# Handing the first pair of each conditional part of a two-round MoE loop to the part in front of it

## The chip, the cores and the metric

The kernel runs on one core of a Trainium2 chip. The metric is the device time of one execution in microseconds; the time of a kernel is the median of several runs. TensorE (PE) does the matrix products and the transposes, VectorE (DVE) and ScalarE (ACT) the elementwise work, GpSimd (POOL) issues the indirect transfers (gathers and scatters by a list of row numbers), and SyncE (SP) issues the direct ones.

## The reference, cut to what matters

The input is 2 x 2048 tokens of 512 numbers. A linear-attention layer comes first and then a mixture of experts (MoE): 32 experts, 8 chosen per token, hidden width 192, everything in float32.

```python
# x: [4096, 512] after the attention layer and its residual, layer-normed
logits = x @ wg.T
weights, idx = top_k(softmax(logits), 8);  weights /= weights.sum(-1)
for each (token, expert) of the 8 x 4096, sorted by expert:
    h = silu(x[token] @ w1[expert]) * (x[token] @ v1[expert])     # 512 -> 192
    out[token] += weight * (h @ w2[expert])                       # 192 -> 512
result = x1 + layernorm(out)
```

How many tokens each expert gets is known only while the kernel runs.

## The kernel before, in words

**Blocks and pairs.** The routing writes, for each expert, a list of its tokens. The lists are cut into blocks of 128 tokens of one expert, and two blocks make a *pair*. The tiles of a pair carry `s` = 0 or 1 for its two blocks. Round 1 has 24 pairs (`NP1`) that are known before the attention is finished; round 2 has up to 120 (`NP2`). The pairs of round 2 are numbered from 0 here.

**`prepare` (L666 to L689)** gets a pair ready. For each of its two blocks SP reads the expert's number (L671) and issues the weights: `w1t` (L674, 768 KB) and `w2t` in two pieces (L675 and L676, 256 and 128 KB). Each has three buffers per block (`NR` = 3), so that the load for pair n waits until pair n-3 has been computed. POOL gathers the 128 token rows into `xg` (L679; four buffers, which are two pairs). PE turns them with four transposes into PSUM, `px` (L685; two buffers), and DVE copies them to SBUF as `xgT` (L687; six buffers).

**`run_pair` (L691 to L729)** computes it. In the records each float32 matrix product counts as two PE instructions. For each block there are 8 PE instructions for `pgu` (L698), then Silu on ACT (L701) and the product `hh` on DVE (L702). Three transposes `ph` (L710) and one copy `hT` (L712) serve both blocks. `py` (L715 four instructions, L719 four) is the second product. ACT scales it by the routing weight (`ysb`, L723) and POOL adds the rows to the accumulators in HBM with an indirect transfer (L724).

**Parts.** Round 2 is cut into parts of 104, 8, 2, 2, 2 and 2 pairs (`PARTS`, L77). Part 0 always runs; each later part sits in an `If` on the number of pairs, `np2`, nested in the one before (L759 to L763). In the profiled execution 138 pairs run in all, 24 in round 1 and 114 in round 2: parts 0, 1 and 2. `second_round` (L749) prepares its first pair, and then for each pair prepares the next one and runs the present one. The first pair of a part has no pair in front of it within the part. So `prepare` of pair 104 is the first thing in the body of part 1, and that of pair 112 the first in part 2.

**Order of the work.** SP's order is the order of the program (`manual_schedule`, L664). For the other engines the framework fixes the order when the kernel is compiled: it goes through a stretch of code, takes for each engine the work that stands earliest in the program among what it reckons to be ready, and lets later work fill in where the earlier is not. The body of an `If` is planned as a stretch of its own, and nothing is moved into it or out of it. On the chip each engine then works strictly in this order, and waits where its next instruction is not ready. There is no common barrier at an `If`: each engine reads `np2`, compares and goes on.

**The end.** After the last part the final stage (L767 to L789) reads both accumulators, normalizes, adds `x1` and stores.

Of the kernel before, what the change touches and what calls it, by code (L numbers as in the profile page):

```python
# [8 lines left out]
F32 = mybir.dt.float32  # L9
# [8 lines left out]
P = 128  # L18
# [5 lines left out]
def linear_attention_then_moe(  # L24
# [24 lines left out]
    C = HID // P  # L49
# [23 lines left out]
    NP2 = (NB - N1 + 1) // 2  # L73
# [3 lines left out]
    PARTS = [(NT * K // BS - N1) // 2, 8, 2, 2, 2, 2]  # L77
# [6 lines left out]
    xn_d = dram.tile([NT + P, HID], F32, name="xn_d")  # L84
# [562 lines left out]
    with ExitStack() as mctx:  # L647
        plan = mctx.enter_context(tc.tile_pool(name="plan", bufs=1))
# [4 lines left out]
        hp = pairs.enter_context(tc.tile_pool(name="hp", bufs=3))  # L653
# [9 lines left out]
        w2v = w2r.rearrange("r (c h) -> (r c) h", c=FC)  # L663
        pairs.enter_context(tc.manual_schedule(engines={mybir.EngineType.SP}))  # L664

        def prepare(r, cols, tid, wt, load, xsrc):  # L666

            xgTs = []
            for s, c0 in enumerate(cols):
                w1t, w2t = w1b[s][r], w2b[s][r]  # L670
                ld = nc.sync.value_load(load[:, c0 : c0 + 1], min_val=0, max_val=2 * E - 1)  # L671
                ex = ld & (E - 1)
                skip = {"cond": ld < E, "bounds_check": "skip_entire_dma"}
                nc.sync.dma_start(w1t, wgu[bass.ds(ex * P, P), :], **skip)  # L674
                nc.sync.dma_start(w2t[:, 0, :], w2v[bass.ds(ex * F + s * FR, P), :], **skip)  # L675
                nc.sync.dma_start(w2t[s * FR : (s + 1) * FR, 1, :],  # L676
                                  w2v[bass.ds(ex * F + (1 - s) * P, FR), :], **skip)
                xg = xg_p.tile([P, HID], F32, tag="xg", name="xg")
                nc.gpsimd.indirect_dma_start(  # L679
                    out=xg, out_offset=None, in_=xsrc,  # L680
                    in_offset=bass.IndirectOffsetOnAxis(ap=tid[:, c0 : c0 + 1], axis=0),
                )
                px = ps_a.tile([P, C, P], F32, tag="xt", name="px")
                for c in range(C):
                    nc.tensor.transpose(px[:, c, :], xg[:, c * P : (c + 1) * P], ident)  # L685
                xgT = hp.tile([P, C, P], F32, tag="xgT", name="xgT", bufs=6)
                nc.vector.tensor_copy(xgT, px)  # L687
                xgTs.append(xgT)
            return xgTs  # L689

        def run_pair(r, cols, tid, wt, load, xgTs):  # L691

            hh = hp.tile([P, 2, F], F32, tag="hh", name="hh")
            for s, xgT in enumerate(xgTs):
                w1t = w1b[s][r]
                pgu = ps_a.tile([P, F2], F32, tag="gu", name="pgu")
                for c in range(C):
                    nc.tensor.matmul(pgu, xgT[:, c, :], w1t[:, c * F2 : (c + 1) * F2],  # L698
                                     start=(c == 0), stop=(c == C - 1))
                hs = hp.tile([P, F], F32, tag="hs", name="hs")  # L700
                nc.scalar.activation(hs, pgu[:, :F], AF.Silu)  # L701
                nc.vector.tensor_mul(  # L702
                    hh[:, s, :].rearrange("p (k c) -> p c k", c=FC),
                    hs.rearrange("p (c k) -> p c k", c=FC),
                    pgu[:, F:].rearrange("p (c k) -> p c k", c=FC),
                )
            hf = hh.rearrange("p s f -> p (s f)")
            ph = ps_a.tile([P, 3, P], F32, tag="ht", name="ph", bufs=1)
            for c in range(3):
                nc.tensor.transpose(ph[:, c, :], hf[:, c * P : (c + 1) * P], ident)  # L710
            hT = hp.tile([P, 3, P], F32, tag="hT", name="hT")
            nc.vector.tensor_copy(hT, ph)  # L712
            py = [ps_a.tile([P, HID], F32, tag="y", name=f"py{s}") for s in range(2)]
            for s in range(2):
                nc.tensor.matmul(py[s], hT[:, 2 * s, :], w2b[s][r][:, 0, :],  # L715
                                 start=True, stop=False)
            for s in range(2):
                rows = slice(s * FR, (s + 1) * FR)
                mm = nc.tensor.matmul(py[s], hT[rows, 1, :], w2b[s][r][rows, 1, :],  # L719
                                      start=False, stop=True)  # L720
            for s, c0 in enumerate(cols):
                ysb = hp.tile([P, HID], F32, tag="ysb", name="ysb")
                nc.scalar.activation(ysb, py[s], AF.Copy, scale=wt[:, c0 : c0 + 1])  # L723
                sc = nc.gpsimd.indirect_dma_start(  # L724
                    out=acc_d[s][:, :],
                    out_offset=bass.IndirectOffsetOnAxis(ap=tid[:, c0 : c0 + 1], axis=0),
                    in_=ysb, in_offset=None, compute_op=ALU.add,
                )
            return mm, sc  # L729

        done = []
        for i in range(NP1):
            pair = (i % NR, (i, NP1 + i), *(a[:, 0, :] for a in round1[:3]))
            done.append(run_pair(*pair, prepare(*pair, xn_d[: SNAP * TB, :])))
# [6 lines left out]
        np2 = plan.tile([P, 1], I32, name="np2")  # L741
        nc.vector.tensor_copy(np2, round2[3])
        np2 = nc.values_load(np2[:1, :], min_val=0, max_val=NP2)

        def pair2(i):
            g, jj = divmod(i, GP2)
            return (NP1 + i) % NR, (jj, GP2 + jj), *(a[:, g, :] for a in round2[:3])

        def second_round(i0, n):  # L749
            ready = prepare(*pair2(i0), xn_d[:, :])  # L750
            for i in range(i0, i0 + n):
                if i % 3 == 0 and i // 3 < NTILE:
                    t = i // 3
                    nc.sync.dma_start(x1_sb[:, t, :], x1_d[t * P : (t + 1) * P, :])
                now, ready = ready, prepare(*pair2(i + 1), xn_d[:, :]) if i + 1 < i0 + n else None
                run_pair(*pair2(i), now)

        second_round(0, PARTS[0])
        with ExitStack() as asked:  # L759
            for k in range(1, len(PARTS)):  # L760
                i0 = sum(PARTS[:k])
                asked.enter_context(tc.If(np2 > i0))
                second_round(i0, PARTS[k])  # L763
        pairs.close()


# [63 lines left out]
```

## Time and profile before

| | |
|---|---|
| time, median of 3 runs | 2855.16 us (2854.49 to 2856.72) |
| the profiled execution's own time | 2861.29 us |
| its span | 2859.5 us |
| mean granted clock of TensorE | 0.966 |
| PE busy over the span | 2645.8 us (93%) |
| first transposes of the MoE | 1342.5 us from the span's start |
| last pair's `py` begins | 2768.76 us |
| first read of the final stage | 2780.68 us |

The profile is of one execution. Positions are microseconds from the start of its span. In the view in order of time a row has start, duration, engine, line, operation, tile written and tiles read, count, and in brackets the idle time in front of it with what ended it. In the view of stretches a row has the stretch, its length, then the busy time and number of instructions of PE, PE's weight loads, DVE, ACT and POOL, the granted clock of PE, the busy share of the DMA engines, and GB/s. In the view of one line's instructions a row has the count and the shortest, median and longest duration in ns.

### The profile page before, as it was taken

Reading aid. Unit: us, or ns where it says so; the run is one execution under the profiler, and the core shown is the slowest. Engines: PE = TensorE matmul, PEld = TensorE weight load, DVE = VectorE, ACT = ScalarE, POOL = GpSimd, SP = SyncE. Lnnn points to the kernel's source line nnn. Section 1 sums busy time; section 2 is a strip of 40 time slices with the busy share of each in tenths; the row PEclk is TensorE's granted clock in tenths of the full one; section 3 lists DMA queues with packets and bytes.
Section 4 is the critical chain, followed back from the end, with each engine's and each line's share of the span. In section 5 each row is a group of like instructions: output and inputs, shape, how many; then the busy total and the mean of one; then the engine's idle time right before and its main releaser. Section 6 shows DMA issues by size and latency. Waiting matters only on the chain. (4 is left out here: it accounts for less than half of the span.)

```text
span 2859.5 us, 29618 instructions
## 1 busy us (share of the span) xinstructions
PE 2645.8 (93%) x8443; PEld 1310.7 (46%) x8443; DVE 1061.4 (37%) x2432; ACT 674.8 (24%) x1208; POOL 1059.9 (37%) x891
## 2 busy tenths in 40 slices
PE   8999999998999999998779899999999999999850
PEld 3434444444444444444435455555555555555420
DVE  5334544546533536554412222222222222222217
ACT  4332222213331313221211112121212121212114
POOL 1100223122320122223455555555555555554426
PEclk9999999999999999999889999999999999999985
DMA  3291211212111212123647899989787988685548
GB/s 112 86 329 51 68 52 52 68 52 67 37 56 45 71 34 71 53 71 114 161 102 175 212 268 257 274 200 254 165 214 160 314 194 199 137 194 114 104 87 323
DMA packets 179290, 399.83 MB, mean 140 GB/s; under 512 B 29413, under 2 KB 30438, under 8 KB 178610
## 3 DMA queue, kind: packets, MB, share of 16 engines
q0 software_dynamic: 70144, 145.31, 25.1%
q1 hardware_dynamic: 101602, 237.55, 24.9%
q10 hardware_dynamic: 7376, 15.02, 1.4%
q8 instruction: 70, 1.15, 0.2%
q14 instruction: 98, 0.80, 0.1%
HBM read 488.74 MB, written 116.66 MB: 212 GB/s over the span
## 5 line engine op out<-in xcount | busy, mean ns | idle before, releaser
L698 PE MATMUL pgu<-w1t,xgT 128*128 128x384 f32 x2208 | 780.0, 496 | 3.5 <-issue 2.4
L724 POOL DMA_INDIRECT acc_d<-ysb,tid x276 | 441.9, 1601 | 503.8 <-ACT ysb L723 389.5
L203 POOL DMA_INDIRECT list_d<-tw,pi x256 | 252.2, 985 | 979.6 <-DVE pi L201 556.2
L698 PEld LDWEIGHTS pgu<-w1t,xgT 128*128 128x128 f32 x2208 | 399.5, 191 | 327.2 <-issue 109.3
L552 PE MATMUL pq<-xlT,wq_sb 128*128 128x512 f32 x1024 | 463.1, 598 | 1.2 <-DVE sq L559 1.2
L584 PE MATMUL acc<-m,sq 128*128 128x512 f32 x1024 | 463.0, 597 | 0.0
L702 DVE TENSOR_TENSOR hh<-hs,pgu 128x192 f32<-128x192 f32 x276 | 97.3, 355 | 975.9 <-ACT hs L701 838.2
L723 ACT ACTIVATE ysb<-py,wt 128x512 f32<-128x512 f32 x276 | 176.5, 684 | 783.4 <-PE py L719 731.8
L679 POOL DMA_INDIRECT xg<-xn_d,tid x276 | 274.9, 996 | 119.0 <-PE px L685 64.0
L552 PEld LDWEIGHTS pq<-xlT,wq_sb 128*128 128x128 f32 x1024 | 190.7, 190 | 241.5 <-issue 230.8
L584 PEld LDWEIGHTS acc<-m,sq 128*128 128x128 f32 x1024 | 189.1, 190 | 239.6 <-issue 239.1
L715 PE MATMUL py<-w2t,hT 128*128 128x512 f32 x552 | 266.4, 605 | 2.1 <-issue 2.1
L555 ACT ACTIVATE qe<-pq,nbq_sb 128x512 f32<-128x512 f32 x128 | 87.8, 686 | 514.6 <-PE pq L552 509.0
L687 DVE COPY xgT<-px 128x512 f32<-128x512 f32 x276 | 188.3, 683 | 43.6 <-PE px L685 41.3
L559 DVE SCALAR_TENSOR_TENSOR sq<-pq,bq_sb,qe 128x512 f32<-128x512 f32 x128 | 95.8, 748 | 286.0 <-ACT qe L556 285.9
L685 PE MATMUL px<-ident,xg 128*128 128x128 f32 x1104 | 174.2, 284 | 29.1 <-DMA xg<-xn_d,tid 26.7
L701 ACT ACTIVATE hs<-pgu 128x192 f32<-128x192 f32 x276 | 90.3, 330 | 363.2 <-PE pgu L698 336.7
L685 PEld LDWEIGHTS px<-ident,xg 128*128 128x128 f32 x1104 | 135.9, 147 | 56.9 <-issue 32.0
L715 PEld LDWEIGHTS py<-w2t,hT 128*128 128x128 f32 x552 | 107.5, 196 | 109.2 <-issue 74.0
L719 PE MATMUL py<-w2t,hT 64*128 64x512 f32 x552 | 157.1, 642 | 0.0
L710 PE MATMUL ph<-ident,hh 128*128 128x128 f32 x414 | 100.5, 298 | 51.3 <-DVE hh L702 51.2
L469 PE MATMUL pk<-wk_sb,xlT 128*128 128x512 f32 x256 | 119.7, 607 | 0.0
(185 smaller groups left out, 1844.8 us busy)
## 6 DMA issues: line engine op xcount, KB each, us to landing
w1t<-in_wgu_dram SPq DMA_DIRECT2D x276, 768.0 KB
w2t<-in_w2r_dram SPq DMA_DIRECT2D x276, 256.0 KB
w2t<-in_w2r_dram SPq DMA_DIRECT2D x276, 128.0 KB
nb<-nr_d SPq DMA_DIRECT2D x128, 256.0 KB
acc_d<-zero SPq DMA_DIRECT2D x6, 2048.0 KB
xb<-in_x_dram SPq DMA_DIRECT2D x32, 256.0 KB
xr<-in_x_dram SPq DMA_DIRECT2D x32, 256.0 KB
wo<-in_woT_dram SPq DMA_DIRECT2D x32, 256.0 KB
```

The costliest lines, as they stand in the source:

```text
L203: nc.gpsimd.indirect_dma_start(out=list_d[:, :], out_offset=bass.IndirectOffsetOnAxis(ap=pi[:, k : k + 1], axis=0), in_=tw[:, k, :], in_of ...
L469: nc.tensor.matmul(pk, xlT[:, c, :], wk_sb[:, c, :], start=(c == 0), stop=(c == C - 1))
L552: nc.tensor.matmul(pq, wq_sb[:, c, h * P : (h + 1) * P], xlT[:, c, :], start=(c == 0), stop=(c == C - 1))
L584: nc.tensor.matmul(pa[s], a[:, s * P : (s + 1) * P], ms[h], start=(h == 0), stop=(h == H - 1))
L679: nc.gpsimd.indirect_dma_start(out=xg, out_offset=None, in_=xsrc, in_offset=bass.IndirectOffsetOnAxis(ap=tid[:, c0 : c0 + 1], axis=0),)
L685: nc.tensor.transpose(px[:, c, :], xg[:, c * P : (c + 1) * P], ident)
L687: nc.vector.tensor_copy(xgT, px)
L698: nc.tensor.matmul(pgu, xgT[:, c, :], w1t[:, c * F2 : (c + 1) * F2], start=(c == 0), stop=(c == C - 1))
L715: nc.tensor.matmul(py[s], hT[:, 2 * s, :], w2b[s][r][:, 0, :], start=True, stop=False)
L719: mm = nc.tensor.matmul(py[s], hT[rows, 1, :], w2b[s][r][rows, 1, :], start=False, stop=True)
L723: nc.scalar.activation(ysb, py[s], AF.Copy, scale=wt[:, c0 : c0 + 1])
L724: sc = nc.gpsimd.indirect_dma_start(out=acc_d[s][:, :], out_offset=bass.IndirectOffsetOnAxis(ap=tid[:, c0 : c0 + 1], axis=0), in_=ysb, in_ ...
```

## The change

`prepare` gets an argument `into`: the two tiles that receive the turned token rows, in place of two from the rotating `xgT`. Two pairs of such tiles, `ahead`, of 2 KB per partition each, are allocated in the pool `plan`, which stays open to the end. `second_round` no longer prepares its own first pair. It is handed the pair that is ready, and in its last turn it prepares the first pair of the *next* part into `ahead[k % 2]` before it runs its own last pair. That `prepare` stands in the body of the part in front, outside the `If` of the part that will use it. It holds all the instructions of `prepare`: two reads of the expert's number and six weight transfers on SP, two gathers on POOL, eight transposes on PE and two copies on DVE. The first pair of part 0 is prepared where it was. The last part that runs now prepares a pair as well, which no part then computes, if there is a next part at all.

```diff
-        def prepare(r, cols, tid, wt, load, xsrc):
+        def prepare(r, cols, tid, wt, load, xsrc, into=None):
...
-                xgT = hp.tile([P, C, P], F32, tag="xgT", name="xgT", bufs=6)
+                xgT = into[s] if into else hp.tile([P, C, P], F32, tag="xgT", name="xgT", bufs=6)
...
-        def second_round(i0, n):
-            ready = prepare(*pair2(i0), xn_d[:, :])
+
+        ahead = [[plan.tile([P, C, P], F32, name=f"ahead{k}{s}") for s in range(2)] for k in range(2)]
+
+        def second_round(k, ready):
+            i0, n = sum(PARTS[:k]), PARTS[k]
             for i in range(i0, i0 + n):
                 if i % 3 == 0 and i // 3 < NTILE:
                     t = i // 3
                     nc.sync.dma_start(x1_sb[:, t, :], x1_d[t * P : (t + 1) * P, :])
-                now, ready = ready, prepare(*pair2(i + 1), xn_d[:, :]) if i + 1 < i0 + n else None
+                now, ready = ready, None
+                if i + 1 < i0 + n:
+                    ready = prepare(*pair2(i + 1), xn_d[:, :])
+                elif i + 1 < NP2:
+                    ready = prepare(*pair2(i + 1), xn_d[:, :], ahead[k % 2])
                 run_pair(*pair2(i), now)
-
-        second_round(0, PARTS[0])
+            return ready
+
         with ExitStack() as asked:
-            for k in range(1, len(PARTS)):
-                i0 = sum(PARTS[:k])
-                asked.enter_context(tc.If(np2 > i0))
-                second_round(i0, PARTS[k])
+            ready = prepare(*pair2(0), xn_d[:, :])
+            for k in range(len(PARTS)):
+                if k:
+                    asked.enter_context(tc.If(np2 > sum(PARTS[:k])))
+                ready = second_round(k, ready)
```

## The prediction

> **What bounds the kernel now.** The page comes first. PE is busy for 93% of the span, so only what shortens PE's work or its idle time counts. Next is the view in stretches around the two places where a part ends and the next begins.
>
> ```profile
> 2637.51:2648.20 10.69, 9.28 (x28) 3.63 (x26) 1.27 (x3) 1.92 (x4) 3.12 (x2) 1.00 0.42 56
> 2648.20:2658.04 9.84, 0.00 (x0) 0.00 (x0) 0.00 (x0) 1.26 (x2) 7.00 (x6) 0.75 0.64 114
> 2658.04:2670.49 12.45, 12.23 (x48) 8.46 (x49) 5.16 (x9) 0.66 (x2) 5.32 (x6) 0.79 0.40 124
> 2699.14:2718.12 18.98, 18.98 (x71) 10.31 (x70) 4.80 (x10) 3.85 (x8) 6.97 (x5) 1.00 0.53 84
> 2738.55:2747.79 9.24, 0.00 (x1) 0.00 (x0) 0.00 (x0) 1.26 (x2) 6.72 (x6) 0.68 0.63 117
> 2747.79:2759.06 11.27, 10.44 (x38) 6.80 (x38) 4.03 (x7) 0.66 (x2) 0.27 (x1) 0.81 0.15 44
> ```
>
> Inside a part PE has no idle time: 18.98 of 18.98 us for two pairs, so 9.49 us a pair. At the boundaries (2648.20 and 2738.55) it does nothing for 9.84 and 9.24 us, and then runs at a mean clock of about 0.8. The rows in order of time say what it waits for.
>
> ```profile
> 2647.06 1.13 PE L719 MATMUL py<-w2t,hT 64*128 64x512 f32 x4
> 2649.18 1.56 POOL L724 DMA_INDIRECT acc_d<-ysb,tid  x1 [4.32 <-ACT ysb L723]
> 2651.04 1.56 POOL L724 DMA_INDIRECT acc_d<-ysb,tid  x1 [0.30 <-issue]
> 2652.91 1.02 POOL L679 DMA_INDIRECT xg<-xn_d,tid  x1 [0.30 <-issue]
> 2654.23 0.98 POOL L679 DMA_INDIRECT xg<-xn_d,tid  x1 [0.30 <-issue]
> 2658.04 3.87 PE L685 MATMUL px<-ident,xg 128*128 128x128 f32 x16 [9.86 <-DMA xg<-xn_d,tid]
> 2661.71 3.54 PE L698 MATMUL pgu<-w1t,xgT 128*128 128x384 f32 x8
> 2665.08 0.38 PE L685 MATMUL px<-ident,xg 128*128 128x128 f32 x2
> 2665.30 2.75 PE L698 MATMUL pgu<-w1t,xgT 128*128 128x384 f32 x8
> 2670.49 1.88 PE L715 MATMUL py<-w2t,hT 128*128 128x512 f32 x4
> ...
> 2743.26 1.01 POOL L679 DMA_INDIRECT xg<-xn_d,tid  x1 [0.30 <-issue]
> 2747.79 4.04 PE L685 MATMUL px<-ident,xg 128*128 128x128 f32 x16 [9.24 <-DMA xg<-xn_d,tid]
> 2751.62 5.54 PE L698 MATMUL pgu<-w1t,xgT 128*128 128x384 f32 x16
> 2759.06 1.98 PE L715 MATMUL py<-w2t,hT 128*128 128x512 f32 x4
> ...
> 2768.76 1.96 PE L715 MATMUL py<-w2t,hT 128*128 128x512 f32 x4 [0.70 <-issue]
> ```
>
> The chain at 2648 is: `py` of pair 103 ends, ACT scales, POOL issues two scatters, and only then the gathers, since POOL works in order. The first gather starts at 2652.91 and has landed by 2658.04, 5.13 us later (4.53 at the second boundary). The 16 transposes are those of pairs 104 and 105. Weights are no part of it: the rows of SP in order of time show loads for pair 106 at 2646.30, so SP is long past the `If`.
>
> **The change, part by part.** *Reference.* I write py(n) for the start of `py` of pair n. Before: py(101) 2627.75, py(103) 2645.17, py(104) 2670.49, py(105) 2681.44, py(106) 2689.64, py(107) 2699.14. From 101 to 107 that is 71.39 us against 6 x 9.49 = 56.94, so boundary 1 costs 14.4 us in all. That is the ceiling there.
>
> *`prepare` of pair 104 moved into part 0.* On SP its loads come in the same order as before, so nothing is moved past anything. On POOL its two gathers now stand in front of the scatters of pairs 101 to 103. There POOL has room: between 2607 and 2649 it waits 3 to 6 us in front of each pair of scatters. Without that cover they would cost two rows of 0.98 us plus 0.30 each, 2.6 us. On DVE two copies of 0.69 us fall where it is mostly idle. On PE eight transposes enter the tail of part 0, which had none. With them py(102) should come one full period after py(101), at 2637.24 (before 2637.51). Then 12 `pgu` instructions follow where there were 8: steady rows give 7.0 us from `py` to their end, and the old tail gives 1.94 us from there to the next `py`. So py(103) is at 2646.2, and its end at 2649.2 instead of 2648.19: **1.0 us later**, with the scatters and gathers behind it.
>
> *What PE finds in part 1.* `pgu` of pair 104 has tokens and weights, so 8 instructions can run at once, to 2652.1. The next question decides the case: where the transposes of pair 105 stand in PE's order. In the program they come before `run_pair(104)`, so they go first once the planner reckons the gather landed. What it reckons is seen in the old part 1: it put two transposes of pair 106 between the two `pgu` groups of pair 104, although pair 106 comes *after* `run_pair(104)` in the program, and its gathers were the fifth and sixth of the body. It thinks gathers quick. Now the gathers of 105 are the first of the body, and I take their transposes to stand after some 8 to 10 `pgu` instructions, within the second group. PE then stops there until the gather of 105 lands. That gather stands behind the scatters of pair 103 as the gather of 104 did: 2652.91 + 1.0 + 4.9 (between 4.53 and 5.13) = 2658.8. **This is the wait that takes the place of the old one**; behind it PE holds the rest of pair 104, and ACT, DVE and POOL its results.
>
> *Sum at boundary 1.* After a stop of 6 us or so I expect the slow clock again. The old row has 3.54 us for 8 `pgu` behind the wait against 2.75 for the next 8, and 16 transposes took 3.87. So from 2658.8: eight transposes in two groups 1.8, the remaining 6 to 8 `pgu` 3.1, then 1.94 to `py`: py(104) = 2665.6, a gain of 4.9. Three steady periods on, py(107) is at 2694.1, or 2694.8 if no `pgu` of 105 slipped in front of py(104); before 2699.14. **Gain 4.65 us** (4.3 to 5.0).
>
> *Boundary 2.* The tail is again 1.0 us longer, so the gather of 113 starts at 2744.3 and lands at 2749.0 (4.53 us, plus some tenths for the weights of pair 114, which are now under way). With the same 1.8 + 3.1 + 1.94, py(112) = 2755.9 against 2759.06: 3.2 gained. Then the waste: pair 114 is prepared and never computed. Its weights and gathers run beside other work (the DMA share is 0.15 there). If that cover were missing, two gathers would cost POOL 2.6 us. Its eight transposes lie partly in PE's waits for `hh` and `hT` at the tail; bounds 0 and 1.0 us, I take 0.5, so py(113) - py(112) = 10.2 (before 9.70), py(113) = 2766.1, **gain 2.7**. The end hangs on pair 113's scatters, so it moves with it.
>
> *Entering the part.* The branch now has less idle time around it.
>
> ```profile
> L759 PEldq COMPARE_BRANCH  x4: 65/142/3689, 2646.7 to 2772.8; - x4
> ```
>
> The two that go on into a body took 92 and 65 ns, while earlier `py` instructions were still in the array; I count 0.1 us each, inside the roundings. The 3689 ns one is the jump over the parts not asked for, at 2768.9. If each entry cost that, the wait for the gather would still cover it in this case.
>
> *Memory.* The tiles take 8 KB per partition of `plan` and move what is allocated behind it, the weight buffers too. The first weights wait for the attention's last product (a 23.2 us wait of SP that ends at 1335). A loss there is hardly possible, as all that lay there is free by then, and a gain is capped, as PE's first transposes wait for the gathers that POOL starts at 1336.1. Bounds -2 and 0 us, I take 0.
>
> *Total.* 4.65 + 2.7 = **7.3 us**. The profiled execution took 2861.29 us, its span 2859.5 and 1.8 around it; that is 6.1 us over the median, without idle time of another kind at the boundaries that I can see. So I take the gain off the median: 2855.2 - 7.3 = **2847.9 us**, -0.26%. About 0.2%, or 5.7 us, is what a measurement of this kernel can tell from no change.
>
> *A rule against it.* The Trainium skill, "TensorE: Matmul & The Clock Gate", Part 1, says that an idle window of about 3.4 us drops PE to half clock, and that it needs about 3.4 us of sustained work to come back. The rows agree in kind: clock 0.75 and 0.68 in the idle stretches, 0.79 and 0.81 after. By that rule a stop cut from 9.8 to 6 us wins nothing of the slow start, about 1.7 us a boundary as an estimate from the page; my sum has the slow start from the rows already and stays as it is.
>
> **The rivals.** *A2, the planner puts the transposes of 105 behind all 16 `pgu`.* Then they run to 2655 while the gather is under way. py(104) = 2658.8 + 1.8 + 1.94 = 2662.5 and py(107) 2691.7, a gain of 7.4; at boundary 2 it is 2749.0 + 1.8 + 1.94 + 10.2 = 2762.9, a gain of 5.9. Total 13.3: **2841.9 us**. Against it: the two early transposes of 106.
>
> *B, they stand behind py(104)*: the stop is gone. The old second boundary has 7.44 us from the first `pgu` to `py`, so py(104) = 2649.3 + 7.44 = 2656.7. With 3.0 of `py`, 1.5 for transposes and copy of 105, 7.44 again and 0.8 for other transposes, py(105) = 2669.4 and py(106) = 2678.9, a gain of 10.7. At the second boundary 2747.1 + 3.0 + 1.4 + 7.44 + 0.5 = 2759.4, a gain of 9.3. Total 20: **2835.2 us**. This needs a planner that knows of the scatters in front.
>
> *C, they stand in front of all of pair 104*: only the copy and half of the transposes are saved. py(104) = 2658.8 + 2.0 + 7.44 + 0.7 (slow clock) = 2668.9, and py(106) gains 1.5; boundary 2 loses 0.5. **2854.2 us**, no change. Against it: `pgu` of 104 is ready at once and nothing else is.
>
> *D, slower: the gather of 105 lands much later.* The last weights and the scatters share the DMA engines with it, and every microsecond of lateness goes into PE's stop at both boundaries, since PE stands in the middle of pair 104. My gain of 7.3 is spent when each lands 3.65 us later than I say, 8.5 us after its start. At 7.3 us later the kernel is 7.3 us slower: **2862.5 us**. For it: the DMA share is 0.64 in the idle stretch, and rises if pair 114's weights come there. Against it: the two landings seen, 5.13 and 4.53 us.
>
> **How the numbers follow.** Case A, the sum above, 52%; A2 13%; B 10%; C 12%; D 13%. Within A the clock and the tail can take 2 us either way, so some 7 in 10 of it lie beyond 5.7 us. Faster: 36 + 13 + 10 = 0.59. Same: 15 from A and 12 from C, 0.27. Slower: D and the last of A, 0.14. Range: from 2837.0 (A2 with 5 us of its own for clock, tail and memory; most of B left out) to 2856.0 (C and 2 us; most of D left out), which leaves out some 19%.
>
> **What would show it.** At 2649 a PE row of `pgu` with no wait in front; some 8 to 10 instructions later transposes with a wait of about 6 us for `xg`; py(104) near 2665.6, and py(112) near 2751.2, which is 2755.9 less the gain of boundary 1. The step on the order is wrong if that wait is missing (B), or is the first thing in the body (C). The step on POOL is wrong if the gather does not start 1.9 us after the last scatter of the part in front. The tail's 1.0 us is wrong if py(103) stays at 2645.2.

## The result and the profile after

The changed kernel takes **2853.02 us** (median of 12 runs, 2846.9 to 2856.86); the kernel before took 2854.70 us beside it (median of 12 runs, 2852.82 to 2859.73). The ratio is 0.999, with an interval of 0.9981 to 0.9999. That is 1.7 us, 0.06%, inside the 0.2% that count here as no change. The forecast was 2847.9 us: the time lies in the forecast's range, but about three quarters of the gain are missing. The profiled execution of after took 2853.38 us, with a span of 2851.6.

The first view is that of stretches: stretch, length, busy time and instructions of PE, of its weight loads, of DVE, ACT and POOL, the granted clock of PE, the DMA share, and GB/s. It shows `py` of pair 103, what lies between it and `py` of pair 104, one period behind that, and for the second boundary what lies between `py` of pairs 111 and 112.

```profile
2639.02:2641.97 2.95, 2.95 (x9) 0.95 (x9) 0.00 (x0) 0.00 (x0) 0.00 (x0) 1.00 0.36 64
2641.97:2651.47 9.50, 1.55 (x6) 0.67 (x4) 0.00 (x0) 1.26 (x2) 6.92 (x6) 0.75 0.63 113
2651.47:2661.70 10.23, 10.22 (x35) 6.82 (x36) 3.78 (x7) 0.66 (x2) 3.39 (x5) 0.73 0.33 102
2661.70:2671.19 9.49, 9.49 (x36) 5.15 (x35) 2.40 (x5) 1.93 (x4) 5.04 (x5) 1.00 0.55 99
2730.56:2741.01 10.45, 1.56 (x7) 0.68 (x5) 0.00 (x0) 1.26 (x2) 6.99 (x6) 0.74 0.65 125
2741.01:2750.84 9.83, 9.83 (x35) 6.67 (x36) 3.78 (x7) 0.66 (x2) 0.00 (x0) 0.76 0.09 30
```

Before, PE did nothing for 9.84 and 9.24 us at the two boundaries. Now it works for 1.55 us and then does nothing for the rest of 9.50 and 10.45 us. Behind the stop the clock is 0.73 and 0.76. The rows of before have 0.79 and 0.81, but over longer stretches; over the first 10 us behind the stop it is 0.74 and 0.79 before and 0.72 and 0.76 now, so the start is slow in both kernels. The same rows in order of time say what PE waits for.

```profile
2641.97 1.56 PE L698 MATMUL pgu<-w1t,ahead 128*128 128x384 f32 x4
2643.03 1.55 POOL L724 DMA_INDIRECT acc_d<-ysb,tid  x1 [5.60 <-ACT ysb L723]
2644.89 1.57 POOL L724 DMA_INDIRECT acc_d<-ysb,tid  x1 [0.30 <-issue]
2646.76 1.02 POOL L679 DMA_INDIRECT xg<-xn_d,tid  x1 [0.30 <-issue]
...
2651.47 1.97 PE L685 MATMUL px<-ident,xg 128*128 128x128 f32 x8 [7.95 <-DMA xg<-xn_d,tid]
...
2653.23 5.93 PE L698 MATMUL pgu<-w1t,ahead 128*128 128x384 f32 x12
...
2661.70 1.88 PE L715 MATMUL py<-w2t,hT 128*128 128x512 f32 x4
...
2735.33 1.01 POOL L679 DMA_INDIRECT xg<-xn_d,tid  x1 [0.30 <-issue]
...
2741.01 1.97 PE L685 MATMUL px<-ident,xg 128*128 128x128 f32 x8 [8.89 <-DMA xg<-xn_d,tid]
2742.77 5.54 PE L698 MATMUL pgu<-w1t,ahead 128*128 128x384 f32 x12
...
2750.84 1.88 PE L715 MATMUL py<-w2t,hT 128*128 128x512 f32 x4
```

The first pair of the part finds its tokens (`ahead`) and weights ready, as the change means it to: the 4 instructions at 2641.97 have no wait in front. But the fifth thing in PE's order is the first transpose of the *second* pair, 105, and PE stands there for 7.95 us until the gather of 105 has landed. The other 12 `pgu` of pair 104, which need nothing that is missing, stand behind it. The old wait has not gone: it belongs to another pair and begins 1.56 us later.

**A caution on positions.** py(112) stands at 2750.84, and the forecast gave 2751.2. That is chance. In this execution py(0) began at 1661.18 us, and at 1667.49 in the profile before, so everything here stands 6 to 7 us early for reasons that do not lie at the boundaries. Only differences between positions are used from here on. I read spans of six pairs: **b1** = py(107) − py(101) and **b2** = py(113) − py(107), in which an undisturbed loop takes 6 x 9.49 = 56.94 us, and for b2, at the end of the round, 55.39 as measured in e_whole below.

Three profiles each of the two unchanged kernels give the sum. Their times were 2861.29, 2854.97 and 2855.64 us before, and 2853.38, 2851.76 and 2851.99 us after. In us:

| | before, three profiles | mean | after, three profiles | mean | gain |
|---|---|---|---|---|---|
| b1 | 71.39, 69.86, 71.65 | 70.97 | 69.61, 69.49, 69.17 | 69.42 | 1.54 |
| of it, the stop | 9.86, 9.13, 9.63 | 9.54 | 7.95, 8.43, 8.02 | 8.13 | 1.41 |
| b2 | 69.62, 70.78, 69.95 | 70.12 | 69.61, 68.96, 68.93 | 69.17 | 0.95 |
| of it, the stop | 9.24, 9.30, 9.47 | 9.34 | 8.89, 8.19, 8.02 | 8.37 | 0.97 |
| py(113) to the end | 90.74, 90.97, 90.58 | 90.76 | 91.81, 91.44, 91.32 | 91.52 | −0.76 |

The spans become shorter by about what the stop becomes shorter, 1.4 and 1.0 us, and that is about the work of the four `pgu` in front of it. Other terms cancel: at the first boundary py(103) − py(101) is 1.03 longer, and py(104) − py(103) is 2.40 shorter, 24.90 against 22.50 in the means. Together 1.54 + 0.95 − 0.76 = 1.73 us, which is what the medians show. The start of round 2 varies by more than that: py(0) lies between 1662.23 and 1667.49 in the three profiles of before, between 1660.06 and 1661.18 in those of after. So the agreement is no proof, and a part of the 1.7 us may come from in front of round 2; the boundaries were read because they are what the change touches.

### The profile page after: what moved, and what is told of

The parts are those of the page before. It is cut to its first block, busy times and chain, and to the rows that moved or that the text cites. A ratio compares the mean times of both kernels' runs of the same rounds, so it can differ in the third digit from the quotient of the medians.

```text
span 2851.6 us, 29678 instructions
## 1 busy us (share of the span) xinstructions
PE 2642.3 (93%) x8451; PEld 1308.6 (46%) x8451; DVE 1062.9 (37%) x2434; ACT 674.9 (24%) x1208; POOL 1062.5 (37%) x893
## 5 line engine op out<-in xcount | busy, mean ns | idle before, releaser
L698 PE MATMUL pgu<-w1t,xgT 128*128 128x384 f32 x2176 | 767.6, 496 | 3.6 <-issue 2.5
L698 PEld LDWEIGHTS pgu<-w1t,xgT 128*128 128x128 f32 x2176 | 392.9, 191 | 324.3 <-issue 108.6
```

## The experiments

The theory, W, is that PE's fixed order holds the loss: the transposes of pair 105 stand in front of work that is ready, and wait for a gather which cannot start before the last scatters of the part in front. The rivals are that entering a part costs something of its own (E), that handing over one pair is not deep enough (D), that the loss is in PE's order alone, whatever the gather does (P), and that a gather is slow wherever it is waited for (G).

**The transposes of the second pair behind `py` of the first (e_late).** All of the second pair's preparation is planned behind the last product of pair 104. On POOL its gathers still start right behind the scatters of pair 103, at 2649.42 in the rows below.

```diff
                 now, ready = ready, None
+                if k and i == i0:
+                    last = run_pair(*pair2(i), now)[0]
+                    with tc.issue_after(last.ins):
+                        ready = prepare(*pair2(i + 1), xn_d[:, :])
+                    continue
```

> The changed kernel, with one difference: at the head of each conditional part the first pair is run first in the program, and the transposes of the second pair are held behind its last py product in PE's order. Gathers and weights are issued as before. I use two spans: py(101) to py(107), over the first boundary, 71.39 us before and 69.61 changed, and py(107) to py(113), over the second, 69.62 before and 69.61 changed; 56.94 would be six undisturbed pairs. Theory W (the wait for the gather of the second pair took the place of the old one, because its transposes stand after 4 pgu instructions in PE's order while its gather stands behind the scatters of the pair in front): pgu of pair 104 runs through, py(104) comes 3.03 + 7.44 = 10.5 us after py(103) in place of 22.7; the gather has landed about when py(104) ends, so there is little waiting left; first span 60.3 us, second 59.8, and about 2834 us in all, 19 below the changed kernel. Rival E (entering a part costs PE this time in itself, by the branch or fetched code): 22 us between py(103) and py(104) stay, both spans stay near 69.6. Rival G (the gather is slow wherever it is waited for): py(104) comes early, but the wait moves behind it, and the first span stays above 66.

Measured: 2841.4 us (median of 4 runs, 2839.06 to 2841.93), ratio 0.9956 (0.9939 to 0.9973). b1 65.36, b2 60.38. PE and POOL in order of time at the first boundary:

```profile
2641.68 1.96 PE L715 MATMUL py<-w2t,hT 128*128 128x512 f32 x4 [0.70 <-issue]
...
2644.63 5.43 PE L698 MATMUL pgu<-w1t,ahead 128*128 128x384 f32 x16
...
2649.42 1.01 POOL L679 DMA_INDIRECT xg<-xn_d,tid  x1 [0.30 <-issue]
...
2652.05 1.95 PE L715 MATMUL py<-w2t,hT 128*128 128x512 f32 x4 [0.70 <-issue]
...
2656.06 1.61 POOL L724 DMA_INDIRECT acc_d<-ysb,tid  x1 [1.85 <-ACT ysb L723]
...
2657.98 0.98 POOL L679 DMA_INDIRECT xg<-xn_d,tid  x1 [0.30 <-issue]
...
2659.26 1.59 POOL L724 DMA_INDIRECT acc_d<-ysb,tid  x1 [0.30 <-issue]
...
2661.16 0.98 POOL L679 DMA_INDIRECT xg<-xn_d,tid  x1 [0.30 <-issue]
...
2666.21 0.87 PE L685 MATMUL px<-ident,xg 128*128 128x128 f32 x3 [2.72 <-DMA xg<-xn_d,tid]
...
2667.52 2.26 PE L698 MATMUL pgu<-w1t,xgT 128*128 128x384 f32 x4
```

py(104) begins 10.37 us after py(103), where it was 22.25 to 22.68 us in after: that is the 10.5 us of work that W expected, so nothing is left that entering the body could cost. E falls, and W stands. But pair 104 has now become so early that the *next* gathers are late. The gathers of pair 107 stand between and behind the scatters of pair 104 in POOL's order (2657.98 and 2661.16), and PE waits for one of them at 2666.21. That is a new wait of 2.72 us; with 0.63 us for a gather of pair 106 and slow work behind it (4 `pgu` in 2.26 us) it makes up most of the 5 us by which b1 is longer than b2. The second part has only two pairs and so no such wait; its 60.38 us are near W's 59.8. W's 60.3 for b1 was missed by 5 us, and the 65.36 lie just under the 66 that was set as the sign of G. Against G stands that the late gather began only at 2661.16, behind the scatters: it had landed 5.05 us after its own start, no later than others.

**The second pair handed over whole as well (e_two).** Each of the later parts prepares two pairs ahead of the one it runs.

```diff
+            def get(j):
+                if j < NP2:
+                    ready[j] = prepare(*pair2(j), xn_d[:, :], ahead[0][:] if j == end else ahead[1][:] if j > end else None)
...
+                if k or i >= end - 2:
+                    if i == end - 2 and not k:
+                        get(i + 1)
+                    get(i + 2)
+                else:
+                    get(i + 1)
+                run_pair(*pair2(i), ready.pop(i))
```

In part 2 both pairs of `ahead` tiles are written again, for pairs 114 and 115, before pairs 112 and 113 have been computed from them. So these two are computed from the wrong rows, and only the first boundary is read.

> Two pairs are handed over at each boundary in place of one, and each conditional part then prepares two pairs ahead, in the program always in front of run_pair. So the second pair of a part is ready at entry, and it is the third whose transposes stand in front. Theory W: PE's order again has transposes (now of pair 106) after 4 pgu instructions of pair 104, and their gather again stands behind the scatters of pair 103, so the same wait of about 8 us stands there; py(103) to py(104) stays at 22.7 us, first span 69 to 70 us, second likewise. Rival D (one pair is just not deep enough, two would cover the gather's way): py(103) to py(104) falls to about 10.5 us and the first span to about 60.

Measured: 2851.34 us (one run); b1 69.89, the same as after. In order of time:

```profile
2640.64 1.56 PE L698 MATMUL pgu<-w1t,ahead 128*128 128x384 f32 x4
2650.07 1.97 PE L685 MATMUL px<-ident,xg 128*128 128x128 f32 x8 [7.88 <-DMA xg<-xn_d,tid]
2651.83 4.89 PE L698 MATMUL pgu<-w1t,ahead 128*128 128x384 f32 x12
```

Two whole pairs are ready and PE does four instructions of them, exactly as with one. What it waits for is now the gather of pair 106. Depth is not what is missing; whatever the body prepares first is put behind the first four `pgu`. D falls.

**Weights and gathers of the second pair issued in the part in front (e_gather).** Only the eight transposes and two copies of pair 105 (`turn`) stay in the body.

```diff
+                xg = held[s] if held else xg_p.tile([P, HID], F32, tag="xg", name="xg")
...
+                if held:
+                    continue
...
+                if k and i == i0:
+                    ready = turn(held)
+                elif i + 1 < i0 + n:
                     ready = prepare(*pair2(i + 1), xn_d[:, :])
                 elif i + 1 < NP2:
                     ready = prepare(*pair2(i + 1), xn_d[:, :], ahead[k % 2])
+                    prepare(*pair2(i + 2), xn_d[:, :], held=held)
```

> The changed kernel, and in addition the weights and the two gathers of the second pair of each part are issued in the part in front, into two tiles of their own; its transposes stay inside the part. This takes away what the wait is for and leaves the transposes early in PE's order. Theory W: no long wait for xg at the head of the part; transposes of pair 105 run first (about 1.2 us), then pgu of 104; a wait of up to 2 us may remain where the transposes of pair 106 fill in before py(104), since its gather is now the first behind the scatters. py(103) to py(104) 12 to 14 us, first span 60 to 62 us. Rival E (cost of entry itself) and rival P (it is the order on PE alone, whatever the gather does): spans stay near 69.6.

Measured: 2838.59 us (one run); b1 63.07, b2 64.44. In order of time:

```profile
2638.52 1.09 PE L698 MATMUL px<-ident,held 128*128 128x128 f32 x8
2639.44 5.33 PE L711 MATMUL pgu<-w1t,ahead 128*128 128x384 f32 x16
2647.90 1.73 PE L687 MATMUL px<-ident,xg 128*128 128x128 f32 x7 [3.02 <-DMA xg<-xn_d,tid]
2651.72 1.88 PE L728 MATMUL py<-w2t,hT 128*128 128x512 f32 x4
```

The transposes of 105 now come first and wait for nothing. So the stop was the landing of that gather, and what delayed it was the queue of scatters on POOL. The wait moves on once more: the first gather in the body is now that of pair 106, and its transposes stand between the `ph` of pair 104, 3.02 us too early. py(104) comes 16.15 us after py(103). W's 12 to 14 us and 60 to 62 for b1 allowed 2 us for this wait and were too low; E and P, which left both spans near 69.6, fall.

**The second pair's transposes behind all `pgu` of the first (e_mid).** This is the forecast's rival A2 made real; `run_pair` also returns its last `pgu` product.

```diff
+                if k and i == i0:
+                    last = run_pair(*pair2(i), now)[2]
+                    with tc.issue_after(last.ins):
+                        ready = prepare(*pair2(i + 1), xn_d[:, :])
+                    continue
```

> The changed kernel, with the transposes of the second pair held behind the last pgu of the first pair, in place of after 4 of its instructions; gathers as in the changed kernel. This is the case A2 of the prediction. By its steps: pgu runs to 5.5 us after entry, then PE waits some 4 us for the gather, py(104) comes 16.3 us after py(103) (22.68 in the changed kernel), first span 64.0 us, second 63.7. If the order only shifts the wait and wins nothing, py(104) stays near 22; if the wait is much longer than the gather's 4.7 us from issue to landing allow, above 18.

Measured: 2844.72 us (one run); b1 65.28, b2 65.24. In order of time:

```profile
2641.23 5.43 PE L698 MATMUL pgu<-w1t,ahead 128*128 128x384 f32 x16
...
2651.14 1.76 PE L685 MATMUL px<-ident,xg 128*128 128x128 f32 x7 [4.37 <-DMA xg<-xn_d,tid]
...
2655.46 2.01 PE L715 MATMUL py<-w2t,hT 128*128 128x512 f32 x4
```

The gather lands as before, 5.12 us after its start at 2646.02; the 12 `pgu` that were behind the wait are in front of it, and the stop is 4.37 us instead of 8. py(104) comes 17.18 us after py(103), where A2 had 16.3. Moving twelve instructions in front of the eight transposes in PE's order is worth 69.42 − 65.28 = 4.1 us at the first boundary and 3.9 at the second, more than the whole change.

**Without the pair that nobody computes (e_nowaste).** Part 2, the last that runs, does not prepare pair 114.

```diff
+            ready = ready or prepare(*pair2(i0), xn_d[:, :])
...
-                elif i + 1 < NP2:
+                elif k < 2:
```

> The changed kernel, but pairs are handed over only at the first two boundaries; part 2, the last that runs here, prepares nothing for a part behind it, and later parts prepare their own first pair. So the weights, two gathers, eight transposes and two copies of pair 114 fall away. The prediction has them at 0.5 us (0 to 1.0). Expected: first span unchanged at 69.6 us, second 68.6 to 69.6. If the waste is what spent the second boundary's gain (2.7 us forecast, 0.0 seen), the second span falls to about 67.

Measured: 2847.21 us (one run); b1 68.11, b2 67.48. In order of time at the second boundary, from the end of `pgu` of pair 112 on:

```profile
2744.76 0.27 PE L710 MATMUL ph<-ident,hh 128*128 128x128 f32 x1
2744.87 1.46 PE L698 MATMUL pgu<-w1t,xgT 128*128 128x384 f32 x4
2746.16 0.38 PE L710 MATMUL ph<-ident,hh 128*128 128x128 f32 x2
2746.38 1.46 PE L698 MATMUL pgu<-w1t,xgT 128*128 128x384 f32 x4
2747.67 1.88 PE L715 MATMUL py<-w2t,hT 128*128 128x512 f32 x4
...
2755.33 1.96 PE L715 MATMUL py<-w2t,hT 128*128 128x512 f32 x4 [0.70 <-issue]
```

From the first `ph` of pair 112 to py(113) this is 10.57 us. In after, with the eight transposes of pair 114 in the gap, it is 2759.79 − 2748.14 = 11.65. The waste costs 1.08 us on PE. The other 0.6 us by which b2 is shorter are a shorter stop (8.13 against 8.37) and 12 `pgu` in 5.25 us against a mean of 5.62; b1 differs by 1.3 us too, with the same order of work, so part of this run's gain is chance.

**No boundary at all (e_whole).** The kernel before with all 114 pairs in part 0.

```diff
-    PARTS = [(NT * K // BS - N1) // 2, 8, 2, 2, 2, 2]
+    PARTS = [(NT * K // BS - N1) // 2 + 10, 2, 2, 2]
```

> The kernel before, with parts of 114, 2, 2 and 2 pairs, so that for these inputs there is no boundary among the pairs that run; the whole computation is done. This measures what the two boundaries cost in all. By the steady rows: first span 6 x 9.49 = 56.94 us, second 4 x 9.49 + 9.76 + 7.66 = 55.4; 28.7 us less than before, about 2826. If the boundaries cost more than the rows show there (say by a disturbed start of what follows), the whole gain is larger than the spans' sum; if some of it is given back at the end, smaller.

Measured: 2827.45 us (median of 4 runs, 2824.88 to 2829.93), ratio 0.9912 (0.9896 to 0.9929). b1 is 56.96 and b2 55.39. Against 70.97 + 70.12 the two boundaries cost 28.7 us together; that is the ceiling for any change of this kind, and the change got 2.5 of it. (This is no kernel to use as it is: it always runs 114 pairs.)

**Both waits of W answered (e_best).** As e_gather, and the body's own first preparation, that of pair 106, is planned behind `py` of pair 104.

```diff
+                if k and i == i0:
+                    ready = turn(held)
+                    last = run_pair(*pair2(i), now)[0]
+                    continue
+                with tc.issue_after(last.ins) if k and i == i0 + 1 else nullcontext():
                     ...
                         ready = prepare(*pair2(i + 1), xn_d[:, :], ahead[k % 2])
+                        prepare(*pair2(i + 2), xn_d[:, :], held=held)
```

> Both remedies together: the weights and gathers of the second pair of a part are issued in the part in front, as in the run with the gathers moved, and the transposes of the third pair are held behind the last py product of the first, so that they wait for no gather either. If the waits of PE for a gather are what is left of the boundary, py(103) to py(104) is 3.03 of py, about 1 of transposes, 7.2 to py: 11.2 us, then full periods; first span 58.1 us (69.61 in the changed kernel), second 57.6 (69.61). That is 23.5 us less than the changed kernel, about 2829.5, and 25 less than before. If something else holds the boundary (slow clock after any pause, the weights of the pairs behind, scatters falling behind the gathers on POOL), one of the spans stays above 60.

Measured: 2831.93 us (median of 5 runs, 2828.81 to 2833.52) against 2854.84 us of before (9 runs), ratio **0.9916** (0.9902 to 0.9930). b1 58.42, b2 57.87. The view of stretches from the end of py(103) to the end of py(104), and from py(111) to py(112), and then the rows in order of time:

```profile
2645.57:2657.44 11.87, 11.87 (x45) 6.60 (x44) 2.91 (x6) 2.26 (x5) 8.67 (x8) 1.00 0.65 135
2722.97:2734.84 11.87, 11.87 (x45) 6.60 (x44) 2.91 (x6) 2.25 (x5) 7.00 (x6) 1.00 0.61 133
```

```profile
2645.57 1.09 PE L698 MATMUL px<-ident,held 128*128 128x128 f32 x8
2646.50 5.33 PE L711 MATMUL pgu<-w1t,ahead 128*128 128x384 f32 x16
...
2654.57 1.88 PE L728 MATMUL py<-w2t,hT 128*128 128x512 f32 x4
2656.38 1.13 PE L732 MATMUL py<-w2t,hT 64*128 64x512 f32 x4
2657.44 1.09 PE L687 MATMUL px<-ident,xg 128*128 128x128 f32 x8
```

PE is busy for 11.87 of 11.87 us, no row waits for a gather, and the clock stays at 1.00 through both boundaries. py(104) comes 11.95 us after py(103), of which 9.49 are a period. Of the 28.7 us the two boundaries keep 116.29 − 112.35 = 3.9. This kernel beats both others, by 0.84% of the time before, and it still prepares pairs at the end that nobody computes.

**Two more profiles of each unchanged kernel (before_2, after_2, before_3, after_3)**, to see what of b1 and b2 repeats.

> The kernel before once more, for a second profile. The boundary spans come from one execution each, and PE's clock after a wait did not come back at the same point in three executions with the same order (12 pgu instructions behind the wait took 5.93, 4.89 and 4.60 us). Theory K (the clock's return shifts a boundary span by 1 to 2 us from execution to execution): first span 70 to 72, second 68 to 71, while the wait for the gather stays within 0.5 us of 9.86 and 9.24. Otherwise the spans repeat to 0.2 us.

> The changed kernel once more, for a second profile. Theory K: both spans between 67.5 and 70.5 us, with the wait for the gather within 0.5 us of 7.95 and 8.89; the difference comes from the instructions right behind the wait. Otherwise both repeat at 69.6.

> The kernel before, for a third profile. As for the second: by theory K first span 70 to 72 us, second 68 to 71; otherwise both repeat to 0.2 us.

> The changed kernel, for a third profile. As for the second: by theory K both spans between 67.5 and 70.5 us; otherwise both repeat at 69.6.

Measured: 2854.97, 2851.76, 2855.64 and 2851.99 us (one run each); the spans are in the table of the first section. The stops of one kernel at one boundary lie within 0.2 to 0.9 us of each other; three of the eight new ones differ from the first profile's by 0.7 to 0.9 us, more than the 0.5 expected. What follows them repeats less well. Two profiles of the *same* kernel before, in order of time at the first boundary, the second profile first and then the third:

```profile
2651.05 1.97 PE L685 MATMUL px<-ident,xg 128*128 128x128 f32 x8 [9.13 <-DMA xg<-xn_d,tid]
2653.28 1.60 PE L685 MATMUL px<-ident,xg 128*128 128x128 f32 x8 [0.26 <-DMA xg<-xn_d,tid]
2654.72 2.75 PE L698 MATMUL pgu<-w1t,xgT 128*128 128x384 f32 x8
```

```profile
2651.69 3.89 PE L685 MATMUL px<-ident,xg 128*128 128x128 f32 x16 [9.63 <-DMA xg<-xn_d,tid]
2655.37 4.02 PE L698 MATMUL pgu<-w1t,xgT 128*128 128x384 f32 x8
```

The same 8 `pgu` take 2.75 us in the one and 4.02 in the other; b1 is 69.86 and 71.65, the first just under the 70 to 72 expected. A difference of 1 to 2 us between single profiles at a boundary is therefore no evidence of anything, and I compare means of three, or differences of 4 us and more.

All spans together, in us:

| kernel | py(104) − py(103) | b1 | b2 | time |
|---|---|---|---|---|
| before (mean of three profiles) | 24.90 | 70.97 | 70.12 | 2854.7 |
| after (mean of three profiles) | 22.50 | 69.42 | 69.17 | 2853.02 |
| e_two | 21.55 | 69.89 | not read | 2851.34 |
| e_nowaste | 21.18 | 68.11 | 67.48 | 2847.21 |
| e_mid | 17.18 | 65.28 | 65.24 | 2844.72 |
| e_late | 10.37 | 65.36 | 60.38 | 2841.4 |
| e_gather | 16.15 | 63.07 | 64.44 | 2838.59 |
| e_best | 11.95 | 58.42 | 57.87 | 2831.93 |
| e_whole | 9.49 | 56.96 | 55.39 | 2827.45 |

The times follow b1 + b2, but for e_late and e_gather: there py(0) stands at 1662.95 and 1658.31 us, and these 4.6 us, far from the boundaries, turn the order of the two.

## Why the prediction was right in kind and wrong in size

**What held.** The case named as likeliest is the one that came: a wait for the gather of pair 105 takes the place of the old one, with pair 104 cut in two by it.
- *POOL.* The gather starts 1.87 us after the last scatter of the part in front begins (forecast 1.9), and has landed 4.71, 5.20 and 4.79 us later in the three profiles, a mean of 4.90 (forecast 4.9). After py(103) it is 12.45 us (forecast 12.6). At the second boundary 5.68, 4.97 and 4.80, mean 5.15; forecast 4.7.
- *The tail of part 0.* py(103) − py(101) grew from 17.42 to 18.45 us: the forecast's 1.0.
- *Behind the boundary*, py(105) follows a full period after py(104): 9.49, as forecast.
- *The branch.* In the view of the line of the `If` the two entries cost nothing that can be seen (e_late shows it best), and the row for the jump over what was not asked for is unchanged at 3.7 us. That row is no cost of 3.7 us shown: it begins at 2759.94, while PE works on py(113) up to 2762.81, and the four other engines take the same jump in 67 ns or less.

```profile
L766 PEldq COMPARE_BRANCH  x4: 65/142/3705, 2640.2 to 2763.9; - x4
```

- *The forecast's case D*, the late landing, did not come, nor its cases B and C in the order of the kernel as given.

**The step that failed** is "I take their transposes to stand after some 8 to 10 `pgu` instructions". They stand after **4**. The place is read from the rows; why the planner chose it is inferred. It seems to think gathers quick, as the prediction read from the two early transposes of pair 106, and quicker than that row allowed to say: there they were the fifth and sixth gathers of the body, and here they are the first two. The consequence in the forecast's own terms, for the first boundary of the profile of after:

| term from the landing to py(104) | forecast | measured |
|---|---|---|
| eight transposes | 1.8 | 1.76 |
| the remaining `pgu`, to the end of the last | 3.1 (6 to 8 of them) | 5.93 (12 of them) |
| from there to `py` | 1.94 | 2.54 |
| sum | 6.84 | 10.23 |

With the landing 0.15 us early the miss on py(104) − py(103) is 22.68 − 19.4 = 3.3 us; the mean of three gives 3.1, and it stays, since the periods behind are full ones. (It equals the 4.65 − 1.54 us by which the gain at b1 fell short, because two terms of 0.4 us cancel: the single profile of before, from which the forecast started, had a b1 0.4 above the mean of three, and the forecast allowed 0.4 too much behind py(104).) The 5.93 us are two things: four to six more instructions, and each of them slow. At full clock 12 `pgu` take 4.14 us (the row of pair 113 in after). Of the 3.1 us missing at this boundary the count alone is some 1.75: with 4 instructions in front b1 gains 1.54 and with 16 (e_mid) 70.97 − 65.28 = 5.69, so 9 would have given about 3.3, an estimate between the two. The other 1.35 us are the clock and the last term. The last term, 1.94, is the old tail's, where no transposes stood between the `ph`; in the steady loop, where they do, it is about 2.5 us, and that row should have been taken.

**Boundary 2** had 2.7 forecast and 0.95 measured. The same step costs it 2.9 us: py(112) − py(111) falls from 24.01 to 22.78 in the means, by 1.2, where the forecast's positions have it fall from 23.52 to 19.4, by 4.1. The tail in front is longer by the forecast's 1.0 (py(111) − py(109) 17.42 and 18.45). Given back is 1.25 us, since four `pgu` of pair 113 slip in front of py(112): py(113) − py(112) is 8.95, and the forecast had 10.2. *The waste* of pair 114 was taken at 0.5 with an upper bound of 1.0; it is 1.08.

**The end** was counted at nothing, and py(113) to the end is 0.76 us longer in after (the three values on each side do not overlap). Some 0.2 us lie in front of the first read of the final stage and 0.6 behind it. The kernels of the experiments range from 89.97 to 92.58 there, e_whole without any waste has the largest value, and the cause is not settled.

**Memory** was taken at 0, with a gain of up to 2. The first transposes of the MoE begin at 1342.49, 1339.84 and 1343.51 us in the three profiles of before and at 1339.46, 1339.02 and 1339.14 in those of after, which looks like a gain of 2.7. But e_late and e_nowaste, with the same new tiles, begin at 1341.58 and 1342.00, and e_whole, which has none, at 1341.04. Over the four profiles without the tiles the mean is 1341.7, over the seven with just these tiles 1340.0. No effect of the new tiles is shown, and it is not excluded; a kernel with the tiles and the old order would tell, and none was run. It would touch the 1.7 us of the whole change, not what was read at the boundaries.

**The reference.** The gain was taken off the median, not off the profiled execution, and that was right: of the 8 us between the two profiled spans, 6.3 were there at py(0).

**The chances.** 0.59 stood on faster by more than 0.2%, 0.27 on no change. It was no change. The prediction had case C (transposes in front of all of pair 104) as the way to a zero; what came lies between C and A, at four instructions of sixteen. The range held it, partly by luck: its upper end was set by C, not by this case. A place in PE's order that a planner chooses was an unknown over all of 0 to 16, and the prediction treated it as known to within one group of eight.

## What to carry to other kernels

When the first work behind a boundary is made ready, PE waits for the second, unless the order of the instructions lets the first go through whole: ask not only what is ready but what stands in front of it on an in-order engine. Moving a gather in front of the scatters that delay it, and moving the transposes that wait behind the work that is ready, are two halves of one change here. By b1 + b2 against before, handing over one pair gave 2.5 us (means of three profiles), with the gather moved as well 13.6, with the transposes moved as well 15.4, and with both 24.8 (one profile each); the measured time of the last is 23 us lower. Compare boundaries by differences between neighbouring events in several profiles, not by positions in one.

## What the runs showed of the hardware that I had not expected

**PE's clock comes back at different moments behind the same stop.** Behind stops of 7.8 to 8.9 us the 12 `pgu` took 5.93, 5.34, 5.42, 5.54, 5.59, 5.72 (after), 4.89 (e_two), 4.60 and 5.25 us (e_nowaste), against 4.14 at full clock. Behind shorter stops the slow clock is there as well. Behind the 2.72 us of e_late the granted clock is 0.57 until py(105), 3.40 us later. Behind the 3.02 and 3.56 us of e_gather it is 0.62 and 0.50 until the next `py`, and seven transposes take 1.73 us against 0.93. In e_best, without such a stop, it is 1.00.

The Trainium skill, "TensorE: Matmul & The Clock Gate", Part 1, says that the activity window of about 3.4 us runs freely and so the number of slow products varies from run to run; the spread above agrees with it in kind. It says that a window's worth of idle time, 3.4 us, brings the half clock; here stops of 2.72 (e_late) and 3.02 us (e_gather) were followed by slow rows too, 4 `pgu` in 2.26 and 1.82 us against 1.46, so a stop below that figure was not safe here.

**A stop that shortens from 9.5 to 8 us gives back about its own difference and no more.** The slow stretch behind it has the same size. Over the first 10 us behind the stop the granted clock is 0.74, 0.84 and 0.69 in the three profiles of before and 0.72, 0.78 and 0.77 in those of after at the first boundary, and 0.79, 0.68, 0.77 and 0.76, 0.76, 0.74 at the second. The means are 0.76 and 0.76, 0.75 and 0.75. To win the slow stretch as well, the stop has to become much shorter: at 2.72 us it was still there, and the waits of 0.70 us in the tails have rows at full speed behind them. Nothing between these two was measured with the same work behind it.
